# Five direct slots and a quarter-packed shared list in a sparse graph-network kernel

## The chip, the cores and the metric

The kernel runs on one core of one Trainium2 chip. The metric is device time in microseconds (us) from launch to end, the median of several runs. The engines are named as the profile names them: PE is TensorE (matrix multiply), PEld its weight loads, DVE VectorE, ACT ScalarE, POOL GpSimd, and SP the queue that issues most DMAs.

## The reference

There are 32 graphs of 512 nodes with 128 features. An adjacency entry is nonzero with chance 1/16, and always on the diagonal. Layer 0 is a normalized graph convolution with residual and layer norm. Layer 1 sums a message over every edge, and the message goes through a layer norm and an exact GELU of its own:

```python
m_j = jnp.einsum('bnd,do->bno', node_features, W1[:D])
m_i = jnp.einsum('bnd,do->bno', node_features, W1[D:])
pre = m_j[:, None, :, :] + m_i[:, :, None, :] + b1
msg = jax.nn.gelu(_layernorm(pre, g1, be1), approximate=False)
agg = jnp.einsum('bijo,bij->bio', msg, adjacency)
upd_in = jnp.concatenate([node_features, agg], axis=-1)
updated = _layernorm(upd_in @ W2 + b2, g2, be2)
```

The result is `_layernorm(x + updated)`. A term with a zero adjacency entry adds nothing, so the kernel computes messages of existing edges alone.

## The kernel before

One graph is one *block* of the program's main loop (not to be confused with a 128 x 128 tile of its adjacency matrix, of which a graph has 16, called *tiles* here). For a tile, each of the 128 rows on the partitions has about eight neighbours among 128 columns, four in each half of 64.

**Direct slots.** `lists` finds for each row and half the eight largest keys, with their indices. The first `SLOTS` = 4 of each half are *direct*: slot `t` of a half is one neighbour for every row. `gathered` brings the index rows into every partition by a broadcast DMA (`raw`), `gathers` turns them into a 0/1 matrix `s` on DVE, `turned` transposes that by DMA into `mt`. A *unit* `(t, q)` handles slot `t` of row chunk `q` against all four column chunks, both halves: 2 x 4 x 128 messages of 128 features.

**Shared places.** The neighbours beyond the direct ones (four kept per half, and up to eight more of the whole tile, found by `more`) are numbered through over the 128 rows of a tile. `counts` makes the running numbers, `spots` makes a 0/1 matrix `sj` that says which row owns which place, `sending` multiplies it with the tile's weights, indices and variances (`sent`), `picks` selects each place's entry and writes index rows to DRAM. A tile has `SHARED * P` = 256 places: two lots of 128. A shared unit handles two row chunks of one lot, 2 x 4 x 128 messages. If a tile had more entries than places, `flag` would be set and `dense_path` would redo the whole work.

**A unit's work.** `pairs` (PE) builds the pre-activation in PSUM (`u`, two buffers): gathers of the features in three bf16 parts (line 869 direct, 887 shared), the deviations times the bias (877, 890), and for shared units also the own rows through `sj` (884). For direct units `sums` (DVE, line 896) adds the own rows and moves the result to SBUF (`m`), which frees the PSUM buffer; for shared units ACT reads PSUM itself. `messages` (ACT, line 929) makes eight GELUs of 128 x 128, `weights` (POOL, lines 912 and 916) makes the weighted scatter matrix `sw`, and `aggregate` (PE, lines 943 and 953) adds the messages up in PSUM (`agg`).

**Order.** Nothing is scheduled by a tool: the order on each engine is the order in which the loop issues. It goes over units two by two. At an even unit `g` PE gets `pairs` of `g` and `g + 1`; at `g + 1` it gets `aggregate` of the two units before those. A block before has 20 units:

```python
order = [(t, q) for t in range(SLOTS - 1) for q in range(C)]
last, more_t = SLOTS - 1, (SLOTS, SLOTS + 1)
order += [(last, 0), (last, 1), (more_t[0], 0), (last, 2), (more_t[0], 1), (last, 3), (more_t[1], 0), (more_t[1], 1)]
```

All other work of a block (`layer0`, `parts`, `lists`, `factors`, `more`, `counts`, `spots`, `sending`, `picks`, `own_edges`, `finish`) is cut into steps by `yield`. `PLAN` gives each step's place by hand, counted in half units from the start of the block's first unit; negative places lie beside the units of the block before. `fetch` issues the DMAs: the index rows three units ahead of a slot's first unit, the compare and the deviation rows two ahead, the transpose one ahead. SP issues in order.

## Time and profile before

| | |
|---|---|
| median of 3 runs | 2945.51 us (2942.2 to 2951.59) |
| the profiled execution | 2950.83 us, span 2949.1 us |
| busy, share of the span | PE 94%, ACT 86%, DVE 83%, PEld 78%, POOL 72% |
| DMA, mean busy share of 16 engines | 42.3% on the main queue |
| mean granted TensorE clock | 0.987 |

The span is the time between the first and the last instruction. Busy shares are averages over the stages of a block; the profile repeats the same pattern for each of the 32 graphs. PE's matmuls overlap, so the time that one takes is best read from the start of a group to the start of the next in the timeline, and not from the mean duration of one.

### The profile page before, as it was taken

How to read it: one execution, taken by the hardware profiler on the slowest of the kernel's cores; microseconds unless marked ns; L12 is line 12 of the kernel's file. 1: busy time of each engine (PE TensorE's matmuls, PEld its weight loads, DVE VectorE, ACT ScalarE, POOL GpSimd, SP SyncE). 2: the span in 40 equal slices, each digit the busy share in tenths (PEclk: the TensorE clock that was granted, in tenths of full speed). 3: DMA queues.
4: the chain of work that ended last, by engine and by line, in shares of the span. 5: the costliest groups of instructions: out<-in, count | busy, mean ns of one | idle time of the engine just before them, and what ended most of it. 6: DMA issues, size and time to landing. Idle time of an engine off the chain costs nothing. (4 is left out here: it accounts for less than half of the span.)

```text
span 2949.1 us, 96041 instructions
## 1 busy us (share of the span) xinstructions
PE 2780.1 (94%) x35393; PEld 2314.2 (78%) x35393; DVE 2441.2 (83%) x9834; ACT 2540.1 (86%) x7841; POOL 2132.8 (72%) x2621
## 2 busy tenths in 40 slices
PE   4999999999999999999999999999999999999996
PEld 2788878788787788787888787788787888787885
DVE  5788988888988888988889888889888889888882
ACT  2888998888888888988888988888989888888885
POOL 3677877777877767776777777778777778776765
PEclk7999999999999999999999999999999999999998
DMA  1444444444443444434444434444434444434442
GB/s 43 91 93 105 103 101 79 99 91 107 106 97 75 93 99 102 109 82 89 100 102 102 101 79 99 93 108 103 101 79 99 89 109 106 100 79 96 91 97 48
DMA packets 593022, 276.09 MB, mean 94 GB/s; under 512 B 456112, under 2 KB 576048, under 8 KB 592544
## 3 DMA queue, kind: packets, MB, share of 16 engines
q1 hardware_dynamic: 592320, 269.41, 42.3%
q8 instruction: 281, 4.60, 0.6%
q14 instruction: 197, 1.61, 0.2%
q0 software_dynamic: 224, 0.46, 0.1%
HBM read 155.45 MB, written 13.63 MB: 57 GB/s over the span
## 5 line engine op out<-in xcount | busy, mean ns | idle before, releaser
L929 ACT ACTIVATE m<-m,r 128x128 f32<-128x128 f32 x4096 | 1267.4, 393 | 39.3 <-DVE m L896 39.3
L912 POOL TENSOR_TENSOR sw<-mt,a_t 128x512 f32<-128x512 bf16 x512 | 617.6, 1220 | 132.3 <-DMA mt<-s 74.1
L896 DVE TENSOR_TENSOR m<-u,ac 128x1024 f32<-128x1024 f32 x512 | 607.0, 1207 | 14.3 <-PE u L877 14.1
L943 PE MATMUL agg<-m,sw 128*64 128x128 f32 x8192 | 514.0, 277 | 5.6 <-ACT m L929 5.0
L943 PEld LDWEIGHTS agg<-m,sw 128*64 128x64 f32 x8192 | 442.7, 137 | 92.0 <-issue 45.5
L869 PEld LDWEIGHTS <-s 64*128 64x128 bf16 x12288 | 365.7, 95 | 138.3 <-issue 63.7
L869 PE MATMUL u<-c,s 64*128 64x128 bf16 x12288 | 434.0, 218 | 13.3 <-DVE s L832 12.7
L686 ACT COPY sent<-pl 128x328 f32<-128x328 f32 x512 | 221.4, 432 | 126.4 <-PE pl L690 66.9
L916 POOL TENSOR_TENSOR sw<-mt,sent 128x512 f32<-128x512 bf16 x256 | 291.3, 1161 | 9.0 <-PE agg L953 6.3
L690 PE MATMUL pl<-a_t,sj 128*128 128x164 f32 x2048 | 293.6, 304 | 0.0
L690 PEld LDWEIGHTS pl<-a_t,sj 128*128 128x128 f32 x2048 | 285.6, 190 | 8.5 <-DVE y L367 8.2
L929 ACT ACTIVATE m<-u,r_s 128x128 f32<-128x128 f32 x1024 | 279.0, 378 | 6.2 <-PE u L890 5.9
L884 PE MATMUL u<-ac,sj 128*128 128x128 f32 x2048 | 273.7, 277 | 0.0
L884 PEld LDWEIGHTS u<-ac,sj 128*128 128x128 f32 x2048 | 263.5, 191 | 12.0 <-DVE a_t L596 5.1
L953 PE MATMUL agg<-m,sw 128*128 128x128 f32 x2048 | 247.5, 277 | 0.0
L953 PEld LDWEIGHTS agg<-m,sw 128*128 128x128 f32 x2048 | 238.7, 192 | 9.2 <-POOL own_u L476 7.9
L887 PE MATMUL u<-c,s 128*128 128x128 bf16 x3072 | 213.3, 219 | 0.0
L523 DVE FIND_INDEX8 idx<-top,key 128x8 uint32<-128x64 f32 x1024 | 210.1, 218 | 0.0
L593 DVE MATCH_REPLACE8 key<-top,key 128x64 f32<-128x64 f32 x1024 | 205.0, 207 | 0.0
L741 POOL TENSOR_SCALAR ve_s<-picked 128x32 f32<-128x32 f32 x32 | 7.9, 248 | 262.0 <-DVE picked L727 262.0
L887 PEld LDWEIGHTS <-s 128*128 128x128 bf16 x3072 | 193.6, 98 | 3.0
L877 PE MATMUL u<-be_d,sd_rows 64*128 64x512 bf16 x1024 | 195.7, 378 | 0.0
(212 smaller groups left out, 5739.6 us busy)
## 6 DMA issues: line engine op xcount, KB each, us to landing
raw<-idx_d SPq DMA_DIRECT2D x256, 256.5 KB
raw<-idx_ds SPq DMA_DIRECT2D x64, 513.0 KB
a_nat<-in_adj_dram SPq DMA_DIRECT2D x32, 1024.0 KB
sd_rows<-sd_d SPq DMA_DIRECT2D x768, 12.0 KB
xs<-in_x_dram SPq DMA_DIRECT2D x32, 256.0 KB
out_dram<-o_sb SPq DMA_DIRECT2D x32, 256.0 KB
sd_d<-sd_p SPq DMA_DIRECT2D x256, 12.0 KB
mt<-s SPq DMA_TRANSPOSE x192
```

What stands on the lines that cost most here:

```text
L523: nc.vector.max_index(idx[:, to, h, :], top[:, to, h, :], half(to, h))
L686: nc.scalar.copy(sent[:, n - 1], pt[:, : SHARED * WIDE].rearrange("p (k w) -> p k w", w=WIDE))
L690: nc.tensor.matmul(pt[:, k * WIDE : (k + 1) * WIDE], sj[:, n, k * P : (k + 1) * P], at[:, n, :], start=True, stop=True,)
L869: nc.tensor.matmul(pu[:, h, c, :], s[halved(h), c, q * P : (q + 1) * P], c3[halved(h), k, c, :], start=(c == 0 and k == 0), stop=False,)
L884: nc.tensor.matmul(pu[:, h, c, :], place, st["ac"][:, q_h, 0, :], start=(c == 0), stop=False)
L887: nc.tensor.matmul(pu[:, h, c, :], s[:, c, q_h * P : (q_h + 1) * P], c3[:, k, c, :], start=False, stop=False)
L896: nc.vector.tensor_tensor(u.rearrange("p h c d -> p (h c) d"), pu.rearrange("p h c d -> p (h c) d"), bcast(state[b]["ac"][:, q, 0, :], 2 * C),
L912: nc.gpsimd.tensor_tensor(sw, mt[:, :, q, :], st["a_t"][:, q, :, :P], ALU.mult)
L916: nc.gpsimd.tensor_tensor(sw, mt[:, :, q_h, :], a, ALU.mult)
L929: nc.scalar.activation(m[:, h, c, :], u[:, h, c, :], AF.Gelu, scale=r[:, k : k + 1])
L943: nc.tensor.matmul(agg[halved(h), c, :], sw[0][:, c, halved(h)], m[:, h, c, :], start=(begin and c == 0), stop=(end and c == C - 1),)
L953: nc.tensor.matmul(agg[:, c, :], sw[h][:, c, :], m[:, h, c, :], start=False, stop=(end and h == 1 and c == C - 1),)
```

## The change

`SLOTS` becomes 5, so a block has 20 direct units. Three entries per half are kept beyond them; their groups stay four wide, the fourth place filled with a value that counts as empty. A tile has `PLACES` = 160 shared places: one full lot of 128 (slot `full`, two units as before) and 32 more (slot `rest`). The 32 places of four tiles lie side by side in the 128 columns of PE's array and become one column chunk; the four chunks make two units with two chunks each, a quarter of a unit's messages. A block has 24 units, and `PLAN` is rewritten for 48 half units.

```diff
-SLOTS = 4
+SLOTS = 5
 KEPT = LIST - SLOTS
-MORE = 2 * KEPT + LIST
-PARTS = MORE // KEPT
-SHARED = 2
+GROUP = 4
+MORE = 2 * GROUP + LIST
+PARTS = MORE // GROUP
+REST = 32
+PLACES = 128 + REST
...
-    "counts": [-3, -3, -2, -2, -2],
-    "own_edges": [7, 18, 22, 30],
-    "spots": [-2, -1, 0, 2, 3, 4, 6, 7, 7, 7],
-    "sending": [8, 9, 9, 9, 9, 9, 9, 9, 9, 9, 9, 9, 9, 9, 9, 9, 9],
-    "picks": [10, 12, 12, 14, 15, 18, 20, 20, 20, 20, 22, 23],
+    "counts": [-5, -1, -1, -1, 2],
+    "own_edges": [6, 10, 17, 32],
+    "spots": [-1, 0, 1, 2, 7, 8, 11, 13, 13, 17],
+    "sending": [20, 25, 25, 25, 25, 25, 25, 25, 25, 25, 25],
+    "picks": [28, 28, 28, 28, 29, 29, 30, 31, 31, 31, 32, 33],
...
+        for k in range(2):
+            pads = at[:, :, P + k * MORE : P + k * MORE + 2 * GROUP].rearrange("p n (h t) -> p n h t", h=2)
+            nc.gpsimd.memset(pads[:, :, :, KEPT:], NEG)
...
-        sj = big.tile([P, C * C, SHARED * P], F32, tag="sj", name=f"sj_{b}")
+        sj = big.tile([P, C * C, PLACES], F32, tag="sj", name=f"sj_{b}")
...
-        for n in range(C * C + 1):
+        for n in range(n_cols // 2 + 1):
             if n:
-                nc.scalar.copy(sent[:, n - 1], pt[:, : SHARED * WIDE].rearrange("p (k w) -> p k w", w=WIDE))
-            if n < C * C:
+                nc.scalar.copy(sent[:, 2 * n - 2 : 2 * n], pt[:, : 2 * WIDE].rearrange("p (k w) -> p k w", w=WIDE))
+            if n < n_cols // 2:
                 pt = bank(f"pl_{b}_{n}")
-                for k in range(SHARED):
...
+                for k in range(2):
+                    col = 2 * n + k
+                    here = slice(k * WIDE, (k + 1) * WIDE)
+                    if col < C * C:
+                        nc.tensor.matmul(pt[:, here], sj[:, col, :P], at[:, col, :], start=True, stop=True)
+                        continue
+                    for q in range(C):
+                        block = q * C + col - C * C
+                        nc.tensor.matmul(
+                            pt[q * REST : (q + 1) * REST, here], sj[:, block, P:], at[:, block, :],
+                            start=True, stop=True, tile_position=(0, q * REST),
+                        )
...
-    last, more_t = SLOTS - 1, (SLOTS, SLOTS + 1)
-    order += [(last, 0), (last, 1), (more_t[0], 0), (last, 2), (more_t[0], 1), (last, 3), (more_t[1], 0), (more_t[1], 1)]
+    last, full, rest = SLOTS - 1, SLOTS, SLOTS + 1
+    order += [(last, 0), (last, 1), (last, 2), (full, 0), (last, 3), (full, 1), (rest, 0), (rest, 1)]
...
+        if t == rest:
+            for c, col in enumerate((2 * q, 2 * q + 1)):
+                for q_h in range(C):
+                    nc.tensor.matmul(
+                        pu[q_h * REST : (q_h + 1) * REST, 0, c, :], st["sj"][:, q_h * C + col, P:],
+                        st["ac"][:, q_h, 0, :], start=(c == 0), stop=False,
+                        tile_position=(0, q_h * REST),
+                    )
+            for c, col in enumerate((2 * q, 2 * q + 1)):
+                for k in range(3):
+                    nc.tensor.matmul(pu[:, 0, c, :], s[:, col, :P], c3[:, k, col, :], start=False, stop=False)
+            nc.tensor.matmul(pu[:, 0, :2], dev[:, 0, :], be_s[:, 2 * q : 2 * q + 2], start=False, stop=True)
+            return pu
...
+            elif t == rest:
+                cols = mt.rearrange("p c q i -> p (c q) i")[:, 2 * q : 2 * q + 2, :]
+                nc.gpsimd.tensor_tensor(
+                    sw[:, :2], cols, st["sent"][:, C * C + 2 * q : C * C + 2 * q + 2, :P], ALU.mult
+                )
...
+        elif t == rest:
+            for c, col in enumerate((2 * q, 2 * q + 1)):
+                nc.tensor.matmul(
+                    agg[:, col, :], sw[0][:, c, :], m[:, 0, c, :], start=False, stop=(end and c == 1)
+                )
```

In `picks` the 32 columns of entries become 20 (16 tiles and four packed chunks). The other lines of `PLAN` are rewritten too: `layer0` begins at -53 instead of -43 and `more` ends at -6 instead of -5.

More of the change, by code (lines that the diff above doesn't have):

```diff
@@ L32 @@
 PLAN = {
-    "layer0": [-43, -41, -39, -39, -38, -37, -36, -34, -34, -33, -32, -31, -30, -30, -29, -28, -27, -27, -27, -27, -26, -24, -20, -18, -16, -3],
-    "lists": [-26, -26, -25, -24, -23, -20, -19, -19, -18, -18, -14, -13, -13, -13, -12, -12, -12, -11, -11, -10, -10],
-    "parts": [-20, -14, -12, -11, -6, -5, -4, -4, -4],
-    "factors": [-12, -11, -10, -8, -7, -7, -7, -6, -5],
-    "more": [-26, -25, -12, -10, -10, -10, -8, -7, -6, -6, -6, -5, -5, -5, -5, -5, -5, -5],
-    "counts": [-3, -3, -2, -2, -2],
-    "own_edges": [7, 18, 22, 30],
-    "spots": [-2, -1, 0, 2, 3, 4, 6, 7, 7, 7],
-    "sending": [8, 9, 9, 9, 9, 9, 9, 9, 9, 9, 9, 9, 9, 9, 9, 9, 9],
-    "picks": [10, 12, 12, 14, 15, 18, 20, 20, 20, 20, 22, 23],
-    "finish": [43, 44, 45, 50, 53, 55, 55, 60, 62, 69, 70, 79, 80],
+    "layer0": [-53, -51, -49, -49, -49, -47, -46, -45, -44, -43, -42, -42, -39, -39, -38, -37, -36, -36, -35, -35, -34, -27, -25, -24, -22, -5],
+    "lists": [-32, -32, -32, -23, -23, -20, -20, -18, -18, -18, -18, -18, -18, -18, -18, -16, -16, -13, -11, -9, -7],
+    "parts": [-10, -9, -8, -6, -4, -4, -4, -3, -2],
+    "factors": [-16, -15, -14, -14, -14, -13, -13, -12, -8],
+    "more": [-25, -25, -22, -14, -13, -13, -13, -11, -11, -11, -11, -10, -10, -7, -7, -7, -7, -6],
+    "counts": [-5, -1, -1, -1, 2],
[3 more added lines that the diff above has]
+    "picks": [28, 28, 28, 28, 29, 29, 30, 31, 31, 31, 32, 33],
+    "finish": [50, 53, 53, 55, 59, 60, 62, 64, 64, 67, 68, 72, 77],
 }
@@ L117, in sparse_path @@
     nc.gpsimd.iota(place_p, pattern=[[0, 1]], base=1, channel_multiplier=1, allow_small_or_imprecise_dtypes=True)
-    n_places = SHARED * P + 2
+    n_places = PLACES + 2
+    n_cols = C * C + C
     place_w = node.tile([P, 3, n_places // 3], F32, tag="t1", name="place_w")
@@ L139, in sparse_path @@
     nc.vector.tensor_add(step_down, step_down, ident_h)
-    place_k = const.tile([P, SHARED], F32, name="place_k")
-    nc.gpsimd.iota(
-        place_k, pattern=[[P, SHARED]], base=1, channel_multiplier=1, allow_small_or_imprecise_dtypes=True
-    )
-    own = slice(0, C * C, C + 1)
-    nth = const.tile([P, KEPT], F32, name="nth")
-    nc.gpsimd.iota(
-        nth, pattern=[[1, KEPT]], base=0, channel_multiplier=0, allow_small_or_imprecise_dtypes=True
+    place_r = const.tile([P, 1], F32, name="place_r")
+    nc.vector.tensor_copy(place_r, place_p)
+    above = const.tile([P, 1], F32, name="above")
+    for k in range(1, P // REST):
+        nc.vector.tensor_scalar(above, place_p, float(k * REST), None, ALU.is_gt)
+        nc.vector.tensor_scalar(above, above, -float(REST), None, ALU.mult)
+        nc.vector.tensor_add(place_r, place_r, above)
+    nc.vector.tensor_scalar(place_r, place_r, float(P), None, ALU.add)
+    own = slice(0, C * C, C + 1)
+    nth = const.tile([P, GROUP], F32, name="nth")
+    nc.gpsimd.iota(
+        nth, pattern=[[1, GROUP]], base=0, channel_multiplier=0, allow_small_or_imprecise_dtypes=True
     )
@@ L609, in counts @@
             nc.scalar.activation(
-                node_i[:, :, h * KEPT : (h + 1) * KEPT], idx[:, :, h, SLOTS:], AF.Copy, bias=float(h * HALF)
+                node_i[:, :, h * GROUP : h * GROUP + KEPT], idx[:, :, h, SLOTS:], AF.Copy, bias=float(h * HALF)
             )
-        nc.scalar.copy(node_i[:, :, 2 * KEPT :], st["idx_m"])
+        nc.scalar.copy(node_i[:, :, 2 * GROUP :], st["idx_m"])
+        for k in range(2):
+            pads = at[:, :, P + k * MORE : P + k * MORE + 2 * GROUP].rearrange("p n (h t) -> p n h t", h=2)
+            nc.gpsimd.memset(pads[:, :, :, KEPT:], NEG)
         nc.gpsimd.tensor_copy(
-            var[:, :, : 2 * KEPT].rearrange("p n (h t) -> p n h t", h=2), top[:, :, :, SLOTS:]
+            var[:, :, : 2 * GROUP].rearrange("p n (h t) -> p n h t", h=2)[:, :, :, :KEPT], top[:, :, :, SLOTS:]
         )
@@ L620, in counts @@
         nc.vector.tensor_reduce(
-            of_part, over.rearrange("p n (g t) -> p n g t", t=KEPT), AX.X, ALU.add
+            of_part, over.rearrange("p n (g t) -> p n g t", t=GROUP), AX.X, ALU.add
         )
@@ L669, in spots @@
                 nc.vector.tensor_copy(
-                    sj[:, 2 * k - 4 : 2 * k - 2, :], pt.pop(k - 2).rearrange("p (n e) -> p n e", n=2)
+                    sj[:, 2 * k - 4 : 2 * k - 2, :],
+                    pt.pop(k - 2)[:, : 2 * PLACES].rearrange("p (n e) -> p n e", n=2),
                 )
@@ L673, in spots @@
                 pt[k - 1] = bank(f"pj_{b}_{k}")
-                nc.tensor.matmul(pt[k - 1], step_down, up_to.pop(k - 1)[:, :, : SHARED * P], start=True, stop=True)
+                nc.tensor.matmul(
+                    pt[k - 1][:, : 2 * PLACES], step_down, up_to.pop(k - 1)[:, :, :PLACES], start=True, stop=True
+                )
             yield
@@ L681, in sending @@
         at = st["a_t"].rearrange("p q c w -> p (q c) w")
-        sent = big.tile([P, C * C, SHARED, WIDE], F32, tag="sent", name=f"sent_{b}")
+        sent = big.tile([P, n_cols, WIDE], F32, tag="sent", name=f"sent_{b}")
         st["sent"] = sent
-        for n in range(C * C + 1):
+        for n in range(n_cols // 2 + 1):
             if n:
-                nc.scalar.copy(sent[:, n - 1], pt[:, : SHARED * WIDE].rearrange("p (k w) -> p k w", w=WIDE))
-            if n < C * C:
+                nc.scalar.copy(sent[:, 2 * n - 2 : 2 * n], pt[:, : 2 * WIDE].rearrange("p (k w) -> p k w", w=WIDE))
+            if n < n_cols // 2:
                 pt = bank(f"pl_{b}_{n}")
-                for k in range(SHARED):
-                    nc.tensor.matmul(
-                        pt[:, k * WIDE : (k + 1) * WIDE],
-                        sj[:, n, k * P : (k + 1) * P],
-                        at[:, n, :],
-                        start=True,
-                        stop=True,
-                    )
+                for k in range(2):
[10 more added lines that the diff above has]
+                        )
             yield
@@ L702, in picks @@
         sent = st["sent"]
-        n_r = SHARED * C * C
-        rank = small.tile([P, SHARED, C * C, PARTS], F32, tag="rank", name=f"rank_{b}", bufs=1)
-        for k in range(SHARED):
+        n_r = n_cols
+        rank = small.tile([P, n_cols, PARTS], F32, tag="rank", name=f"rank_{b}", bufs=1)
+        for cols, place in ((slice(0, C * C), place_p), (slice(C * C, n_cols), place_r)):
             nc.vector.tensor_scalar(
-                rank[:, k], sent[:, :, k, P + 2 * MORE :], place_k[:, k : k + 1], -1.0, ALU.subtract, ALU.mult
+                rank[:, cols], sent[:, cols, P + 2 * MORE :], place, -1.0, ALU.subtract, ALU.mult
@@ L708, in picks @@
             )
-        chosen = node.tile([P, SHARED, C * C, MORE], BF16, tag="idx_r", name=f"chosen_{b}")
+        chosen = node.tile([P, n_cols, MORE], BF16, tag="idx_r", name=f"chosen_{b}")
         picked = small.tile([P, 2, n_r], F32, tag="picked", name=f"picked_{b}", bufs=1)
-        for k in range(SHARED):
-            nc.vector.tensor_tensor(
-                chosen[:, k].rearrange("p n (g t) -> p (n g) t", t=KEPT),
-                bcast(nth, C * C * PARTS),
-                rank[:, k].rearrange("p n g -> p (n g)").unsqueeze(2).to_broadcast([P, C * C * PARTS, KEPT]),
-                ALU.is_equal,
-            )
+        nc.vector.tensor_tensor(
+            chosen.rearrange("p n (g t) -> p (n g) t", t=GROUP),
+            bcast(nth, n_cols * PARTS),
+            rank.rearrange("p n g -> p (n g)").unsqueeze(2).to_broadcast([P, n_cols * PARTS, GROUP]),
+            ALU.is_equal,
+        )
@@ L718, in picks @@
         yield
         for h in range(2):
-            kept = node.tile([P, SHARED, C * C, MORE], F32, tag="xs", name=f"kept_{b}_{h}")
-            nc.vector.tensor_tensor(
-                kept,
-                chosen,
-                sent[:, :, :, P + h * MORE : P + (h + 1) * MORE].rearrange("p n k l -> p k n l"),
-                ALU.mult,
-            )
-            nc.vector.tensor_reduce(picked[:, h, :], kept.rearrange("p k n l -> p (k n) l"), AX.X, ALU.add)
+            kept = node.tile([P, n_cols, MORE], F32, tag="xs", name=f"kept_{b}_{h}")
@@ L728, in picks @@
+            nc.vector.tensor_tensor(kept, chosen, sent[:, :, P + h * MORE : P + (h + 1) * MORE], ALU.mult)
+            nc.vector.tensor_reduce(picked[:, h, :], kept, AX.X, ALU.add)
             yield
             if h == 0:
-                idx_h = small.tile([P, C, SHARED * C], BF16, tag="idx_s", name=f"idx_s_{b}", bufs=1)
-                for k in range(SHARED):
-                    nc.scalar.copy(
-                        idx_h[:, :, k * C : (k + 1) * C],
-                        picked[:, 0, k * C * C : (k + 1) * C * C].rearrange("p (q c) -> p q c", c=C),
-                    )
@@ L736, in picks @@
-        n_i = SHARED * C
+                idx_h = small.tile([P, C, C + 1], BF16, tag="idx_s", name=f"idx_s_{b}", bufs=1)
+                nc.scalar.copy(idx_h[:, :, :C], picked[:, 0, : C * C].rearrange("p (q c) -> p q c", c=C))
+                nc.scalar.copy(idx_h[:, :, C], picked[:, 0, C * C :])
+        n_i = C + 1
         pt = bank(f"pidx_s_{b}")
@@ L741, in picks @@
         nc.gpsimd.tensor_scalar(
-            ve.rearrange("p (k c q) -> p k q c", k=SHARED, c=C),
-            picked[:, 1, :].rearrange("p (k q c) -> p k q c", k=SHARED, c=C),
+            ve[:, : C * C].rearrange("p (c q) -> p q c", c=C),
+            picked[:, 1, : C * C].rearrange("p (q c) -> p q c", c=C),
             1.0 / D,
@@ L748, in picks @@
         )
+        nc.gpsimd.tensor_scalar(ve[:, C * C :], picked[:, 1, C * C :], 1.0 / D, EPS, ALU.mult, ALU.add)
         r = small.tile([P, n_r], F32, tag="r_s", name=f"r_s_{b}")
@@ L763, in picks @@
         n = C * C
-        sd_d = dram.tile([SHARED, 3, n, P], BF16, tag="sd_ds", name=f"sd_ds_{b}")
+        sd_d = dram.tile([3, n, P], BF16, tag="sd_ds", name=f"sd_ds_{b}")
+        sd_e = dram.tile([3, C, P], BF16, tag="sd_dr", name=f"sd_dr_{b}")
         yield
-        for k in range(SHARED):
-            nc.sync.dma_start(sd_d[k].rearrange("k n j -> n k j"), sd_p[k * n : (k + 1) * n])
+        nc.sync.dma_start(sd_d.rearrange("k n j -> n k j"), sd_p[:n])
+        nc.sync.dma_start(sd_e.rearrange("k n j -> n k j"), sd_p[n:])
+        st["sd_dr"] = sd_e
         st["sd_ds"] = sd_d
@@ L816, in gathered @@
             src, n0 = state[b]["idx_ds"], (t - SLOTS) * C
-        n = C * N + PAD
-        raw = onehot.tile([P, 3, n // 3 + 2], BF16, tag="raw", name=f"raw_{b}_{t}", bufs=1)
+        raw = onehot.tile([P, 3, (C * N + PAD) // 3 + 2], BF16, tag="raw", name=f"raw_{b}_{t}", bufs=1)
+        n = (N if t == rest else C * N) + PAD
         s = raw[:, :, : n // 3]
@@ L831, in gathers @@
         s = onehot.tile([P, C * N + PAD], BF16, tag="s", name=f"s_{b}_{t}", bufs=3)
+        n = N if t == rest else C * N
         nc.vector.tensor_scalar(
-            s.rearrange("p (k e) -> p k e", k=3), raw, node_h if t < SLOTS else node_p, None, ALU.is_equal
+            s[:, : n + PAD].rearrange("p (k e) -> p k e", k=3), raw, node_h if t < SLOTS else node_p, None, ALU.is_equal
         )
-        return s[:, : C * N]
+        return s[:, :n]
     def turned(b, t, s):
         mt = onehot.tile([P, C, C, P], BF16, tag="mt", name=f"mt_{b}_{t}", bufs=4)
-        nc.sync.dma_start_transpose(out=mt.rearrange("p c q i -> p (c q) i"), in_=s)
+        nc.sync.dma_start_transpose(out=mt.rearrange("p c q i -> p (c q) i")[:, : s.shape[-1] // P], in_=s)
         return mt
@@ L846, in deviations @@
         st = state[b]
-        srcs = [st["sd_d"][2 * t + h] for h in BOTH] if t < SLOTS else [st["sd_ds"][t - SLOTS]]
+        if t == rest:
+            for k in range(3):
+                nc.sync.dma_start(
+                    rows_t[k * DEV : (k + 1) * DEV, 0, :], st["sd_dr"].rearrange("k c j -> (k c) j")
+                )
+            return rows_t
+        srcs = [st["sd_d"][2 * t + h] for h in BOTH] if t < SLOTS else [st["sd_ds"]]
         for h, src in enumerate(srcs):
@@ L878, in pairs @@
             return pu
+        if t == rest:
+            for c, col in enumerate((2 * q, 2 * q + 1)):
[4 more added lines that the diff above has]
+                        tile_position=(0, q_h * REST),
+                    )
+            for c, col in enumerate((2 * q, 2 * q + 1)):
+                for k in range(3):
+                    nc.tensor.matmul(pu[:, 0, c, :], s[:, col, :P], c3[:, k, col, :], start=False, stop=False)
+            nc.tensor.matmul(pu[:, 0, :2], dev[:, 0, :], be_s[:, 2 * q : 2 * q + 2], start=False, stop=True)
+            return pu
         for h in BOTH:
             q_h = 2 * q + h
-            k = t - SLOTS
             for c in range(C):
-                place = st["sj"][:, q_h * C + c, k * P : (k + 1) * P]
+                place = st["sj"][:, q_h * C + c, :P]
                 nc.tensor.matmul(pu[:, h, c, :], place, st["ac"][:, q_h, 0, :], start=(c == 0), stop=False)
@@ L908, in weights @@
         out_w = []
-        for h in BOTH if t >= SLOTS else BOTH[:1]:
+        for h in BOTH if t == full else BOTH[:1]:
             sw = pair.tile([P, C, P], F32, tag="sw", name=f"sw_{b}_{t}_{q}_{h}", bufs=6)
@@ L912, in weights @@
                 nc.gpsimd.tensor_tensor(sw, mt[:, :, q, :], st["a_t"][:, q, :, :P], ALU.mult)
+            elif t == rest:
+                cols = mt.rearrange("p c q i -> p (c q) i")[:, 2 * q : 2 * q + 2, :]
+                nc.gpsimd.tensor_tensor(
+                    sw[:, :2], cols, st["sent"][:, C * C + 2 * q : C * C + 2 * q + 2, :P], ALU.mult
+                )
             else:
                 q_h = 2 * q + h
-                a = st["sent"][:, q_h * C : (q_h + 1) * C, t - SLOTS, :P]
+                a = st["sent"][:, q_h * C : (q_h + 1) * C, :P]
                 nc.gpsimd.tensor_tensor(sw, mt[:, :, q_h, :], a, ALU.mult)
@@ L923, in messages @@
         n = C * C
-        for c in range(C):
+        for c in range(2 if t == rest else C):
             if t < SLOTS:
                 r, k = st["r"], (t * 2 + h) * n + c * C + q
+            elif t == rest:
+                r, k = st["r_s"], n + 2 * q + c
             else:
-                r, k = st["r_s"], (t - SLOTS) * n + c * C + 2 * q + h
+                r, k = st["r_s"], c * C + 2 * q + h
             nc.scalar.activation(m[:, h, c, :], u[:, h, c, :], AF.Gelu, scale=r[:, k : k + 1])
@@ L949, in aggregate @@
                     )
+        elif t == rest:
+            for c, col in enumerate((2 * q, 2 * q + 1)):
+                nc.tensor.matmul(
+                    agg[:, col, :], sw[0][:, c, :], m[:, 0, c, :], start=False, stop=(end and c == 1)
+                )
         else:
@@ L970, in crowded @@
         nc.vector.tensor_reduce(peak, pt[:1, :P], AX.X, ALU.max)
-        nc.vector.tensor_scalar(flag, peak, SHARED * P + 0.5, None, ALU.is_gt)
+        nc.vector.tensor_scalar(flag, peak, PLACES + 0.5, None, ALU.is_gt)
     made_r, made_s, made_m, made_d = {}, {}, {}, {}
@@ L1020, in gather_two @@
             b, t, q = unit(k)
-            held[k] = pairs(b, t, q, made_s[b, t].rearrange("p (c j) -> p c j", j=N), made_d[b, t])
+            held[k] = pairs(b, t, q, made_s[b, t].rearrange("p (c j) -> p c j", c=C), made_d[b, t])
     def sum_one(k):
@@ L1062, in sparse_path @@
                 ready[k] = (u, m, sw)
-                work += [(key, u, m, h) for h in BOTH]
+                work += [(key, u, m, h) for h in (BOTH[:1] if key[1] == rest else BOTH)]
             if odd:
```

## The prediction

> **What bounds the kernel now.** First the page: who is busy, and whether anything but the steady repetition of blocks matters.

> ```profile
> span 2949.1 us, 96041 instructions
> PE 2780.1 (94%) x35393; PEld 2314.2 (78%) x35393; DVE 2441.2 (83%) x9834; ACT 2540.1 (86%) x7841; POOL 2132.8 (72%) x2621
> PE   4999999999999999999999999999999999999996
> ```

> PE is busy from end to end, at nearly full granted clock. The next view lists the instructions that write `agg_sb`, one for each block, and so gives the period: (2924.8 - 173.3) / 31 = 88.8 us.

> ```profile
> L775 DVE TENSOR_TENSOR agg_sb<-agg,own_u x32: 690/691/693, 173.3 to 2924.8; 128x512 f32<-128x512 f32 x32
> ```

> The windows view of one period shows each engine's load in it.

> ```profile
> 1000.00:1089.20 89.20, 85.55 (x1101) 71.04 (x1100) 76.44 (x306) 78.54 (x244) 65.54 (x81) 1.00 0.47 96
> ```

> The columns after the length are PE, PEld, DVE, ACT, POOL, clock, DMA share, GB/s. PE idles 3.65 us a block, ACT 10.7, DVE 12.8. PE sets the period. "Busy" alone could hide a stalled PE, so I read the starts in PE's timeline (start, duration, instructions):

> ```profile
> 1018.43 1.97 PE L943 MATMUL agg<-m,sw 128*64 128x128 f32 x32
> 1020.33 0.28 PE L760 MATMUL psd_s<-ident,sd_s 128*32 128x128 f32 x1
> ...
> 1050.79 1.05 PE L884 MATMUL u<-ac,sj 128*128 128x128 f32 x8
> ...
> 1052.56 1.05 PE L884 MATMUL u<-ac,sj 128*128 128x128 f32 x8
> ...
> 1054.34 1.95 PE L953 MATMUL agg<-m,sw 128*128 128x128 f32 x16
> 1056.22 1.09 PE L943 MATMUL agg<-m,sw 128*64 128x128 f32 x16
> ...
> 1079.34 0.84 PE L869 MATMUL u<-c,s 64*128 64x128 bf16 x24
> 1080.02 0.38 PE L877 MATMUL u<-be_d,sd_rows 64*128 64x512 bf16 x2
> 1080.23 0.83 PE L869 MATMUL u<-c,s 64*128 64x128 bf16 x24
> 1080.90 0.38 PE L877 MATMUL u<-be_d,sd_rows 64*128 64x512 bf16 x2
> 1081.21 9.18 PE L690 MATMUL pl<-a_t,sj 128*128 128x164 f32 x64
> 1090.32 1.86 PE L943 MATMUL agg<-m,sw 128*64 128x128 f32 x30
> ```

> The groups follow each other without a gap: PE really issues at its rate. From start to start, a direct unit costs 0.89 + 1.90/2 = 1.84, with its share of shape changes 1.9 us; a shared unit 2 x 1.77 (from L884 to the next half's L884) + 1.88 = 5.42 us; `sending` 9.11 us for 32 matmuls (0.285 each; the trace counts an f32 matmul as two).

> **The change, part by part, per block.**

> *PE.* Four more direct units: +7.6. Two shared units fewer: -10.84. The two quarter units: each has eight f32 matmuls of 32 columns, which the trace doesn't show. The nearest row is L943: 32 of 64 columns take the time of 16 full ones (1.90 against 1.88), so two half-wide ones run side by side. Bounds: four side by side, 2 x 0.22 = 0.45 us a unit, or one after the other, 8 x 0.22 = 1.78. I take the first, because of L943. With six bf16 (0.33), the deviation (0.2), two `aggregate` matmuls (0.47) and two shape changes (0.2) a unit costs 1.65, the two +3.3. `sending`: 16 full (4.56) and 16 quarter ones, 1.14 side by side or 4.56 in a row; with shape changes 5.9 instead of 9.11, -3.2. `spots` has 320 instead of 512 columns: eight at 0.31 shrink in proportion at most, -0.8. Sum **-3.9** us (+2.2 with every quarter matmul alone).

> A shape change is seen above: L869 follows L877 in 0.21 us, but L690, with other tiles of the array, follows in 0.31, so a change costs 0.1. [...]

> *ACT.* The rows (ACT's timeline gives 20 direct GELUs in 5.86 us from start to start, 0.293 each, and 16 shared ones in 4.02, 0.251 each):

> ```profile
> L929 ACT ACTIVATE m<-m,r 128x128 f32<-128x128 f32 x4096 | 1267.4, 393 | 39.3 <-DVE m L896 39.3
> L686 ACT COPY sent<-pl 128x328 f32<-128x328 f32 x512 | 221.4, 432 | 126.4 <-PE pl L690 66.9
> ```

> 32 more direct GELUs +9.4; 32 shared ones become 16 + 4, -3.0; 16 `sent` copies become ten, -2.6. **+3.8**.

> *DVE.* Four more L896 (607.0 us in 512) +4.7; one more compare (a quarter of one slot) +0.4; `spots` and `picks` shrink by 3/8 in width: between nothing and -5.0 (L661, L669, L712, L721 and L727, together 13.5 a block); fixed parts remain, so -3.7. **+1.4**.

> *POOL.* Four more L912 at 617.6 / 512 = 1.21, +4.8; eight L916 at 291.3 / 256 = 1.14 become four, -4.6; two of half width between 0.6 and 1.1 each, +1.2; the power on 32 columns (5.4 us; 1.05 on 4) becomes 20 columns, -1.9; two memsets and one extra op +0.6. **+0.1**.

> *DMA and SP.* One more transpose of a quarter, index rows 3.1 to 3.2 MB, 36 instead of 30 deviation issues. At a share of 0.47 this is no bound by itself, but see the rivals.

> Window sums after: PE 81.6, ACT 82.3, DVE 77.8, POOL 65.6. The bound falls from 85.55 to 82.3, 3.2 us. But before, one engine led; afterwards PE and ACT are level, and the engine that is longer changes along the block. So I added the rows pair of units by pair of units, in the order of issue (PE, ACT, DVE, POOL, in us; DVE's last pairs are one entry, halved here; small waits are in PE's rows):

> ```
> before  0  8.5 10.6  7.6  6.4    after  0  4.9 10.0  7.2  9.7
>         1 10.3  7.7  9.2 10.1           1 10.3  5.2  6.1  6.8
>         2 15.5 13.8  7.2  4.1           2  6.8  6.8  6.0  4.6
>         3 10.7  9.8  8.5 10.0           3  8.8  9.1  5.8  4.1
>         4  5.3  4.7  5.5  4.6           4  3.9  5.2  5.0  6.1
>         5  6.1  6.3  6.8  7.2           5  6.9  4.7  5.2  4.1
>         6  4.8  5.2  8.5  3.9           6  9.0 10.6  9.5  3.9
>         7  7.4  8.8  7.4  9.4           7  4.4  6.3  8.6  7.6
>         8  7.4  6.0  7.7  5.6           8  4.1  9.3  7.7  5.2
>         9 11.0  6.0  7.7  4.8           9  9.1  5.0  6.6  2.4
>                                        10  7.4  5.7  4.9  3.4
>                                        11  7.4  4.8  4.9  8.1
> ```

> PSUM's two `u` buffers and five `m` buffers let engines drift apart by a pair or two, so waits even out over some stretch. Taking the largest engine sum in each stretch, averaged over where the cuts fall: with half blocks 88.5 before and 86.7 after; with thirds 90.6 and 88.1. Their mean, 89.55 before, is 0.75 above the measured 88.8; after it is 87.4, or 86.65 with 0.75 taken off. With fifths the sums are 91.4 and 92.4, which speaks against a gain, so I choose a value between, a period of 87.1, **1.7 us less**.

> Start and end (72.8 us until the first unit, the last block's finish) hold the same chains. 32 x 1.7 = 54: the span goes from 2949.1 to 2895. The profiled execution (2950.83) lies 5.3 above the median, so the median goes to 2945.5 - 54 = **2891**.

> **The rivals.** *POOL and the transpose at the seam of two blocks: slower.* There DMA is full (share 1.07 from 1057 to 1069 us: adjacency load, index rows, transpose), and `mt` comes late, in POOL's timeline

> ```profile
> 1066.04 2.30 POOL L912 TENSOR_TENSOR sw<-mt,a_t 128x512 f32<-128x512 bf16 x2 [5.27 <-DMA mt<-s]
> ```

> and in the list of waits, with total, times and longest:

> ```profile
> POOL sw L912 <- DMA mt<-s: 74.1, 18, 6.2
> ```

> Before, pairs 9, 0, 1 give PE 29.8 against POOL's 21.3: the wait, 4.1 on the mean, is covered. After, pairs 11, 0, 1 give PE 22.6, ACT 20.0, and POOL 24.6: no cover. If 4.1 come on every block the period is 91.2, the time 3022; half of it, 2957. It decides from 1.7 us a block. For it: the last pair before the seam is now the two quarter units. Against it: SP may issue earlier than the loop's place, and POOL has slack in pairs 9 and 10.

> *The quarter matmuls don't run side by side: slower.* +6.1 on PE, 87.7 in the window, with the 3.65 idle of before 91.35 against 89.2: 2945.5 + 32 x 2.15 = 3014. L943 speaks against it.

> *The engines even out fully: faster.* 82.3 and no more idle time than the 3.65 of before, 85.95 against 89.2: 2945.5 - 32 x 3.25 = 2841.

> *The alternation eats all: no change.* The fifths say this: 2945.

> That a tile overflows its places, and `dense_path` runs, I exclude: counted from the inputs, the fullest tile needs 142 of 160 places (253 of 256 before).

> **Chances.** Forecast 0.46, evening out 0.12, no change 0.10, seam 0.24, no packing 0.08. Run-to-run spread is 0.3%, about 9 us, which separates faster and slower from no change. The no-change case falls 0.02 to each side, so faster 0.60, same 0.06, slower 0.34. The range reaches from 2830, under the evening-out case, to 3000, into the seam case; the forecast's own range is 2855 to 2930.

> **What would show it.** Right: a period near 87, ACT and PE both near 82 busy, `sending` near 5.9 us from start to start, four quarter matmuls starting within some 0.11 us. Wrong: POOL's wait for `mt` above 1.7 us a block with PE waiting for `sw` (seam); quarter matmuls 0.1 us apart (no packing); PE and ACT waiting in turn for L896 and each other, period near 89 (alternation).

## The result, and the profile after

The changed kernel takes 3042.27 us (median of 4 runs, 3038.05 to 3051.49) against 2946.56 us before on the same chip: 1.0328 times the time, 95% interval 1.0312 to 1.0344. The prediction said 2891, faster; the time lies above its range. The profiled execution took 3041.32 us.

The page's engine line and the instructions that write `agg_sb` (first and last start give the period):

```profile
span 3039.5 us, 104394 instructions
...
PE 2740.4 (90%) x38785; PEld 2194.3 (72%) x38785; DVE 2506.4 (82%) x9973; ACT 2652.4 (87%) x8289; POOL 2128.5 (70%) x2780
```
```profile
L786 DVE TENSOR_TENSOR agg_sb<-agg,own_u x32: 672/678/693, 173.6 to 3015.2; 128x512 f32<-128x512 f32 x32
```

(3015.2 - 173.6) / 31 = 91.7 us a block, 2.9 more than before. The windows view, summed over 24 stretches of one steady block each, first before (89.12 us), then after (92.26 us; the last block is shorter, so the mean of all is 91.7):

```profile
sum 2138.88, PE 2069.09 PEld 1726.73 DVE 1823.55 ACT 1902.12 POOL 1592.22; mean PE 86.21 PEld 71.95 DVE 75.98 ACT 79.25 POOL 66.34
```
```profile
sum 2214.24, PE 2039.77 PEld 1635.04 DVE 1870.52 ACT 1983.67 POOL 1588.58; mean PE 84.99 PEld 68.13 DVE 77.94 ACT 82.65 POOL 66.19
```

ACT, DVE and POOL have the loads that were forecast (82.3, 77.8, 65.6), yet no engine is busy for more than 85 of 92.3 us. Before, PE was at work for all but 2.9 of 89.1. PE's timeline shows what is new (start, duration, instructions, idle time before and what ended it):

```profile
1049.69 3.05 PE L706 MATMUL pl<-a_t,sj 128*128 128x164 f32 x20 [0.26 <-ACT sent L699]
1052.67 1.32 PE L710 MATMUL pl<-a_t,sj 128*32 128x164 f32 x32
1053.92 1.97 PE L980 MATMUL agg<-m,sw 128*64 128x128 f32 x32
...
1061.83 0.28 PE L769 MATMUL psd_s<-ident,sd_s 128*20 128x128 f32 x1 [3.20 <-POOL sd_s L762]
1062.04 3.58 PE L980 MATMUL agg<-m,sw 128*64 128x128 f32 x32
```

The quarter matmuls (L710) run side by side as forecast (sixteen in 1.25 us from start to start). But PE stands for 3.2 us until POOL has made `sd_s`, and the next L980 takes 3.58 instead of 1.97 us. The windows view of four stretches of 3.41 us around it gives the reason (the columns are as in the prediction; the last three are the granted clock, the DMA share, GB/s):

```profile
1055.18:1058.59 3.41, 2.93 (x70) 2.16 (x66) 3.27 (x7) 3.41 (x14) 1.04 (x3) 1.00 0.01 2
1058.59:1062.00 3.41, 0.21 (x2) 0.09 (x1) 3.41 (x25) 2.42 (x8) 3.33 (x3) 1.00 0.10 21
1062.00:1065.41 3.41, 3.41 (x33) 3.28 (x32) 3.41 (x35) 3.23 (x13) 2.50 (x4) 0.50 1.02 216
1065.41:1068.82 3.41, 3.41 (x82) 2.88 (x80) 2.54 (x6) 3.36 (x8) 3.21 (x5) 1.00 0.27 88
```

After a window with PE almost idle (0.21 of 3.41 us busy) the granted clock is 0.50 for one window. PE's waits, first before and then after (total, times, longest):

```profile
PE po L634 <- DVE count_h L626: 31.6, 32, 1.0
PE pidx L534 <- ACT idx_h L528: 24.3, 30, 8.4
```
```profile
PE psd_s L769 <- POOL sd_s L762: 102.6, 32, 3.6
PE pconv L367 <- POOL a_t L330: 30.4, 30, 1.6
PE u L914 <- ACT m L966: 29.6, 31, 1.0
PE pt_x L269 <- ACT x L257: 27.9, 32, 4.9
```

All of PE's waits that come at least ten times add up to 97.5 us before and 234.9 after: 3.05 and 7.34 us a block. Time at half clock is 81 us before, nearly all at the two ends, and 205 after: (205 - 81) / 32 = 3.9 us a block at half rate, 1.9 lost if PE is busy in it, as in the third window above. So, by difference, 88.8 was 85.7 of work and 3.05 of waits; 91.7 is 82.4 of work, 7.34 of waits, 1.9 of clock. The work fell by 3.3, and 6.2 came back as waits and clock.

### The profile page after: what moved, and what is told of

It is laid out like the page before. It is cut to its first block, busy times and chain, and to the rows that moved or that the text cites. A ratio compares the mean times of both kernels' runs of the same rounds, so it can differ in the third digit from the quotient of the medians.

```text
span 3039.5 us, 104394 instructions
## 1 busy us (share of the span) xinstructions
PE 2740.4 (90%) x38785; PEld 2194.3 (72%) x38785; DVE 2506.4 (82%) x9973; ACT 2652.4 (87%) x8289; POOL 2128.5 (70%) x2780
## 3 DMA queue, kind: packets, MB, share of 16 engines
q1 hardware_dynamic: 630080, 279.98, 42.7%
## 5 line engine op out<-in xcount | busy, mean ns | idle before, releaser
L966 ACT ACTIVATE m<-m,r 128x128 f32<-128x128 f32 x5120 | 1571.2, 392 | 48.5 <-DVE m L926 46.6
L926 DVE TENSOR_TENSOR m<-u,ac 128x1024 f32<-128x1024 f32 x640 | 769.2, 1214 | 116.3 <-PE u L895 114.9
L942 POOL TENSOR_TENSOR sw<-mt,a_t 128x512 f32<-128x512 bf16 x640 | 739.1, 1166 | 170.3 <-DMA mt<-s 131.9
L980 PE MATMUL agg<-m,sw 128*64 128x128 f32 x10240 | 695.7, 289 | 1.6 <-POOL sw L942 1.0
L980 PEld LDWEIGHTS agg<-m,sw 128*64 128x64 f32 x10240 | 597.3, 144 | 91.7 <-issue 41.9
L844 DVE TENSOR_SCALAR s<-raw,node_h 128x2052 bf16<-128x2052 bf16 x160 | 202.8, 1268 | 96.2 <-DMA raw<-idx_d 80.7
L526 DVE MAX8 top<-key 128x8 f32<-128x64 f32 x1024 | 170.0, 210 | 1.1
L706 PEld LDWEIGHTS pl<-a_t,sj 128*128 128x128 f32 x1024 | 144.3, 190 | 35.7 <-ACT sent L699 18.8
L914 PE MATMUL u<-ac,sj 128*128 128x128 f32 x1024 | 141.6, 281 | 29.7 <-ACT m L966 29.6
L914 PEld LDWEIGHTS u<-ac,sj 128*128 128x128 f32 x1024 | 129.2, 191 | 50.5 <-ACT m L966 40.4
L367 PE MATMUL pconv<-s,a_t 128*128 128x128 f32 x1024 | 129.4, 281 | 32.6 <-POOL a_t L330 30.4
```

The source lines that it names most:

```text
L526: nc.vector.max(top[:, seq[n], h, :], half(seq[n], h))
L706: nc.tensor.matmul(pt[:, here], sj[:, col, :P], at[:, col, :], start=True, stop=True)
L844: nc.vector.tensor_scalar(s[:, : n + PAD].rearrange("p (k e) -> p k e", k=3), raw, node_h if t < SLOTS else node_p, None, ALU.is_equal)
L914: nc.tensor.matmul(pu[:, h, c, :], place, st["ac"][:, q_h, 0, :], start=(c == 0), stop=False)
L926: nc.vector.tensor_tensor(u.rearrange("p h c d -> p (h c) d"), pu.rearrange("p h c d -> p (h c) d"), bcast(state[b]["ac"][:, q, 0, :], 2 * C),
L942: nc.gpsimd.tensor_tensor(sw, mt[:, :, q, :], st["a_t"][:, q, :, :P], ALU.mult)
```

## The experiments

I followed the changed kernel's twelve blocks from the 14th to the 25th back from wait to wait, with the rule of the profile's chain of waits. Us of one block on the chain:

```
          PE    ACT   POOL   DVE   DMA   of
before   39.2   11.5   4.3   26.9   3.2   88.8
after    18.8   30.0  18.8   12.7   8.5   92.3
```

The rest, some 3.6 us, is SP's issuing and time in which the engine waited for nothing that the profile shows. The shares move by a microsecond or so with the way in which a wait is cut. The same hand-overs come in twelve blocks of twelve: `sent` (ACT), rank, chosen, kept, picked (DVE), the power for `r_s` (POOL, 3.56 us); from there the chain goes to `psd_s` (PE) in ten and on to ACT in eight. At the seam they are POOL's chain to `xb`, DVE's layer norm, POOL's power, ACT's `x`, PE's `pt_x`, again in all twelve. The theories tested: **D**, such serial chains, with queues in order on every engine, set the period; **P** and **A1**, PE or ACT alone does; **the seam**, as in the prediction's first rival; **the clock**.

All runs are given as ratio to the kernel before on the same chip; a difference of 0.01 is 0.92 us a block. Intervals are about 0.002 wide on each side. The changed kernel stands at 1.0328.

**PE's wait and the wait for `mt`.** In three runs the wait for `psd_s` was moved or filled, in a fourth POOL's step behind the wait for `mt` was moved (in e1 the steps of `picks` behind `psd_s` move by up to one half unit too):

```
 e1   yield  before the transpose psd_s, "picks": [28, 28, 28, 28, 29, 29, 31, 31, 32, 32, 32, 33, 33]
 e2   the same yield,                    "picks": [28, 28, 28, 28, 29, 29, 30, 30, 31, 31, 31, 32, 33]
 e3   + for _ in range(12): nc.tensor.matmul(pt, ident_h, be_d..., start=True, stop=True)   # ahead of psd_s
 e4   layer0's step that holds deg ... xb: place -46 -> -47
```

> The changed kernel with one step cut in two: the transpose of the shared deviations (psd_s) stands two half units later (place 31 instead of 29), behind the rows of indices, which stay. Theory A (a new wait: PE stands 3.2 us a block at that transpose, until POOL has made the power of 20 columns, and the clock is halved for a window behind it, which stretches the next aggregate from 1.97 to 3.58 us): both go, 32 x 4.8 = 155 us less, about 2890 us, granted clock back from 0.967 to about 0.985. Theory B (POOL and the late transposed matrices at the seam of two blocks, 131.9 us of waits): no change of more than 10 us, 3042. Theory C (PE and ACT take turns and no place helps): the wait comes back elsewhere, above 3000.

> The same, with the transpose only one half unit later (place 30). Theory A: half a unit is about 1.9 us, so some 1.3 us of the wait are left, too short to halve the clock for long: 32 x 3.5 = 112 us less, about 2930 us. If the clock's part did not belong to the wait, it would be 32 x 1.9 = 61 us less, 2980. Theory B: 3042. Theory C: above 3000.

> The changed kernel with twelve more matmuls of 128 x 512 (bf16, overwritten by the transpose, results unused) in the place where PE waits. They add 2.6 us of work inside a wait of 3.2 us. Theory A in two parts: if idling is what halves the clock, the wait stays and the clock does not fall: 32 x 1.6 = 51 us less, about 2990 us, and the aggregate behind it takes 1.97 us again. If the slow aggregate has another cause, no change, 3042. Theory B: no change. If PE had no time to spare there, 32 x 2.6 = 83 us more.

> The changed kernel with one step of layer0 one half unit earlier (the degree chain on POOL, place -47 instead of -46), so that it stands ahead of the block's first scatter matrix in POOL's order and no longer waits with it for the late transpose. Theory B: what the late transpose costs goes, up to 4.1 us a block, 131 us less, 2911. Theory A: at most the 1.0 us a block that PE waits at the convolution for POOL, 3010 to 3042.

Measured: e1 1.0481, e2 1.0305, e3 1.0349, e4 1.0304. In e2 and e3 the clock is back (110 and 74 us at half rate in all), PE's page time is down to 2720 us in e2, and nothing is gained. In e2 the wait has moved on:

```profile
PE psd L573 <- ACT sd L565: 53.4, 32, 12.8
PE psd_s L770 <- POOL sd_s L762: 41.8, 32, 1.7
PE agg L981 <- POOL sw L943: 36.0, 51, 0.9
```

So in the changed kernel this wait of PE is a symptom; what holds POOL and ACT up stays. e1 lost 1.4 us a block. In its trace SP's issue of the shared deviations waits for ACT for 185.9 us in all instead of 71.0, and PE waits for ACT ahead of `aggregate` for 50.4 us; that these are the cause isn't shown. e4's 0.2 us a block lies within the two intervals: holding `deg` up is at most a small part of what POOL's wait for `mt` costs.

**The loads.** GELUs and matmuls left out:

```
 f1   GELU of half 1, column 3 left out in slots 1 and 2 (8 a block)     h1   in slots 0 to 4 (20)
 f2   for k in range(3) -> range(2) at L887 in slots 1 and 2 (64)        h2   in slots 0 to 4 (160)
 h3   h1 and h2 together
```

> Leaves out 8 of the 160 direct GELUs of a block (half 1, column 3 of slots 1 and 2), 2.34 us of ACT by its row of 0.293 us each; nothing else changes. Theory D (a chain through several engines): followed back from wait to wait over twelve blocks of the changed kernel, the chain lies on ACT for 30.0 us of 92.3, on PE for 18.8, on POOL for 18.8, on DVE for 12.7, in DMA for 8.5; GELUs hold 19.4 us of it, of some 52 us of GELUs in a block, so 37% of what is left out comes back, 0.9 us a block, 28 us, near 3014. Theory P (PE still sets the period, through its own waits): nothing comes back, 3042. Theory A1 (ACT alone is the bound): all comes back, 75 us, near 2967.

> Leaves out the third of the three bf16 matmul terms of the same two slots (64 matmuls a block), 8 units of 0.28 us, 2.24 us of PE; ACT, DVE, POOL and DMA do the same as before. Theory D: these matmuls hold 2.05 us of the chain of 17.8 us in a block, 12%, so 0.3 us a block comes back, 8 us, near 3034. Theory P: all 2.24 us, 72 us, near 2970. Theory A1: nothing.

> As the run with 8 GELUs left out, now in all five direct slots: 20 GELUs a block, 5.9 us of ACT. Theory A1 (ACT is the bound): 5.9 us a block, 188 us, near 2854. Theory P (PE is the bound): nothing, 3042. Theory D (the chain goes back and forth between engines that are all busy for 78 to 85 us of 92, and shortening one leaves a parallel chain through the others): a part, 0 to 1.8 us a block, 2984 to 3042.

> Leaves out the third bf16 term in all five direct slots: 160 matmuls, 5.6 us of PE a block. Theory P: 179 us less, near 2863. Theory A1: nothing. Theory D: close to nothing, 0 to 1 us a block, 3010 to 3042.

> Both omissions at once, 5.9 us of ACT and 5.6 us of PE a block. Theory P: the 5.6 us of PE, no more than with PE's omission alone; theory A1: the 5.9 us of ACT, no more than with ACT's alone. Theory D: clearly more than the two single effects added, since the two parallel chains get shorter together: 3 to 5 us a block, 2880 to 2945.

Measured: f1 1.0322, f2 1.0324, h1 1.0284, h2 1.0317, h3 1.0204. So 5.9 us less on ACT give 0.4 us a block, 5.6 less on PE give 0.1, both 1.1. P and A1 are refuted; D is right in kind (more together than one by one), but not in size: f1 gave 0.06 us a block where 0.9 was expected, and h3 gave less than 3 to 5. In f1 the chain followed back lies on PE for about 30 us and on ACT for under 14 at an unchanged 92.2: several chains are nearly as long as the longest.

**The chains.** The transfer at the seam, and POOL's power:

```
 f3   a_nat kept from the first block; later blocks load [:, 0:1] of it (256 of 1024 KB)
 i1   - rsqrt(r, ve)
      + nc.gpsimd.tensor_copy(r[:, : C * C], ve[:, : C * C])
      + rsqrt(r[:, C * C :], ve[:, C * C :])
 i2   f3 and i1 together
```

> Loads only a quarter of the adjacency (256 of 1024 KB) in every block but the first, so that the transfer that stands ahead of the seam's transpose in the queue takes some 0.9 instead of 3.4 us; the rest keeps the first block's values, and no engine's work changes. Theory D: the load's landing holds 3.2 us of the chain and the transpose behind it 2.3; up to 2.5 us a block comes back, 0.9 if the next chain is that close, so 28 to 80 us, 2962 to 3014. Theories P and A1: nothing, since neither PE nor ACT has less to do.

> Leaves out the power for 16 of the 20 columns of r_s (a copy stands there), so that the step of 3.56 us on POOL, which lies on the chain in twelve blocks of twelve, takes about 1.4 us; ACT, PE, DVE and DMA have the same work, and POOL, busy 66 us of 92, is not short of time. Theory D (serial chains that pass through several engines set the period): a part of the 2.2 us comes back, 0.5 to 2 us a block, 2980 to 3026. Theory L (loads set it: whatever is left is one engine's busy time): nothing, 3042.

> The omission in r_s and the quarter of the adjacency together. The adjacency alone gave 1.35 us a block back (3042 to 3000). Theory D: both chains follow each other in a block, so the effects add or nearly: 2 to 3.3 us a block, 2936 to 2980. Theory L: as the adjacency alone, 3000.

Measured: f3 1.0175, i1 1.0263, i2 1.0120: 1.4, 0.6 and 1.9 us a block. Both chains count, the effects add (2.0 by sum), and no engine but POOL has less to do; i1's whole cut of POOL's step is 2.3 us (3.55 to 0.19 + 1.03) of an engine that idles for 26. SP's waits (after, then f3) and POOL's show one way in which the transfer costs:

```profile
SPq L852 <- DMA a_nat<-in_adj_dram: 84.6, 30, 4.4
...
POOL sw L942 <- DMA mt<-s: 131.9, 51, 9.4
```
```profile
SPq L853 <- DMA a_nat<-in_adj_dram: 13.9, 30, 1.6
...
POOL sw L943 <- DMA mt<-s: 83.5, 51, 9.9
```

The transpose of the new block's first slot is held on SP until the adjacency has landed, in 30 blocks of 32, 2.8 us each. A second way is ACT's own wait for the adjacency (`mask`), 26.6 us after and 10.6 in f3; f3 doesn't part the two.

The hold itself is not new. SP's timeline at the seam, before and then after:

```profile
1055.72 0.51 SPq L273 DMA_DIRECT2D a_nat<-in_adj_dram  x1
...
1056.87 5.13 SPq L840 DMA_TRANSPOSE mt<-s  x1
```
```profile
1085.55 0.40 SPq L280 DMA_DIRECT2D a_nat<-in_adj_dram  x1
...
1093.05 2.04 SPq L852 DMA_TRANSPOSE mt<-s  x1
```

Before, the transpose is issued 1.1 us behind the load and stands on SP itself for 5.1 us where most others take 1.8 to 2.0; in 30 of 31 blocks it ends within 0.1 us of the load's landing. After, it is the eighth DMA issued behind the load in 30 blocks, and SP waits ahead of it for the semaphore that the load counts up. What the hold cost the kernel before, no run shows.

**The clock.** h3 has the clock down for 341 us. With e3's twelve matmuls in it:

> The run with 20 GELUs and 160 matmuls left out a block (3010), with twelve matmuls of no use added where PE waits for psd_s, as in the earlier run with them, so that the clock stays up. That run had 59 windows at half clock, 341 us in all; the kernel before has 81 us of them at its two ends, so (341 - 81) / 32 = 8.1 us a block at half rate, 4.1 us of PE time. If the clock's windows ate what the lighter engines freed: up to 3 us a block, 2915 to 2980. If they lie off the chain: 3010.

Measured: 1.0090 against h3's 1.0204, 1.05 us a block, with 122 us at half clock. The mean clock and span of h3, then of this run:

```profile
core 0: 3014.8 us, clock 0.944
```
```profile
core 0: 2966.2 us, clock 0.980
```

So the halved clock took away part of what the lighter engines had freed. In e3, with the changed kernel's full work on ACT, the same fillers gave nothing.

**One place in the kernel before.** Only the step with the index rows' way to DRAM and `psd_s` moves, three half units earlier:

```
 e5   (kernel before)  picks: [10, 12, 12, 14, 15, 18, 20, ...] -> [10, 12, 12, 14, 15, 15, 20, ...]
```

> The kernel before, with nothing changed but the place of the transpose psd_s, which stands right behind POOL's power as in the changed kernel instead of one step of the plan later. Theory D with the clock gate: PE comes to wait there some 3 us in each block, the window behind is granted half the clock (38 such windows in the changed kernel, 7 in the kernel before), and 2 to 4 us a block are lost, 3010 to 3075, near what the whole change lost. Rival: the wait is filled up elsewhere in the block, 2947.

Measured: 1.0242, 2.2 us a block, though no work changed. The size is as expected, the way is not: PE hardly waits for `psd_s` (7.8 us in all), and the clock stays up (83 us at half rate in all). SP's timeline, before and then with the move, shows another queue:

```profile
1003.08 1.77 SPq L840 DMA_TRANSPOSE mt<-s  x1
1004.90 1.82 SPq L823 DMA_DIRECT2D raw<-idx_d  x2
1016.08 0.28 SPq L497 DMA_DIRECT2D idx_ds<-idx_rs  x1
...
1020.93 2.97 SPq L840 DMA_TRANSPOSE mt<-s  x1
```
```profile
1023.01 1.72 SPq L840 DMA_TRANSPOSE mt<-s  x1
1036.01 0.27 SPq L497 DMA_DIRECT2D idx_ds<-idx_rs  x1
...
1036.62 1.24 SPq L823 DMA_DIRECT2D raw<-idx_d  x2
...
1043.06 1.90 SPq L840 DMA_TRANSPOSE mt<-s  x1
```

The index rows' DMA waits for ACT (SP's L497 behind `m`: 338.4 us in all, 301.5 before) and stands ahead of `raw` now; the next `raw` goes out 13.6 instead of 1.8 us after the transpose, and from transpose to transpose it is 20.05 instead of 17.85 us: the 2.2 us. In the blocks from the 6th to the 28th this stretch is 20.17 instead of 17.84 us on the mean, and no other stretch between two transposes of a block changes by more than 0.4. PE has the same work and the largest load as ever, and one place is enough to let a chain through SP set the period.

**Other places.** Three sets of places for the changed kernel, with the same instructions (nearly every row of `PLAN` changed by a few half units; the third set's `picks` as an example):

```
 k1   "picks": [28, 28, 28, 28, 29, 29, 30, 31, 31, 31, 32, 33] -> [28, 28, 28, 29, 29, 30, 31, 31, 32, 33, 33, 33], ...
```

> The changed kernel with other places in the plan and nothing else: the same instructions, moved by one to eight half units, found by replaying each engine's queue in order with the durations of the two traces and keeping moves that shorten the period. Theory D: the loss sits in the waits between in-order queues, so other places bring it back; the replay, which gives 90.2 us a block for the changed kernel and 87.8 for the kernel before, gives 85.7 here, so 2830 to 2920. Theories P and A1: as much work on PE and on ACT as before, 3042 or close to it.

> The changed kernel with a second set of places, from the replay with its durations corrected by the runs so far (it now gives 92.2 us a block for the changed kernel, 87.8 for the kernel before, which measured 88.8, and 90.9 for the first set of places, which measured 92.2). For this set it gives 88.3. Theory D: 1.5 to 3.9 us a block less than the changed kernel, 2915 to 2995, the upper part the likelier since the replay was too low by 1.3 for the first set. Theories P and A1: 3042.

> The changed kernel with a third set of places, found with the clock's windows in the replay (a window of 3.41 us in which PE is busy for less than half is followed by one at half clock). The replay gives 87.1 us a block, 1.1 less than for the second set, which measured 90.8. Theory D: 1 to 3 us a block less than the changed kernel, 2945 to 3010. If no set of places helps further: near 3018, the second set's time. Should it come out under 2945, it beats the kernel before.

Measured: g1 1.0299, g2 1.0223, k1 1.0244. The best set brings 1.0 us a block back; all three stay behind what I expected of them, and none beats the kernel before. The replay (each engine's queue run through in order, with durations from the traces) had said 85.7, 88.3 and 87.1 us a block before they ran; 92.2, 91.5 and 91.5 were measured in the steady part. So it did not see a large part of what holds these orders up, and which part stays open. In g2 POOL's wait for `mt` is nearly gone:

```profile
POOL sw L951 <- DMA mt<-s: 5.9, 3, 5.0
```

That is 5.9 us in all, against 131.9 on `sw` L942 alone, and still only 1.0 us a block came back.

**All omissions.**

```
 l1   i2, h3 and the twelve matmuls of no use together
```

> All the omissions at once: 20 GELUs and 160 matmuls a block, the power for 16 columns, three quarters of the adjacency, and the twelve matmuls of no use. Theory D with its parts following each other in the block: the 2973 of the run with GELUs, matmuls and fillers less the 59 that power and adjacency gave (3042 to 2983), near 2915. If a load that none of them touches (DVE, 78 us of busy time a block) sets a floor: no lower than 2950.

Measured: 2914.38 us, 0.9894 (0.9872 to 0.9916), 4.0 us a block under the changed kernel. j3 and i2 by themselves gave 2.2 and 1.9. So chains, loads and clock add up in the changed kernel, and DVE at 77.84 us of busy time a block of 88.08 isn't the floor yet.

## Why the prediction was wrong

*PE's work.* Right within some 0.6 us. Predicted -3.9 a block, about -3.3 by the difference above. From the starts: a quarter unit 1.12 us plus its share of `aggregate`, 1.6 (predicted 1.65); `sending` 6.3 (5.9); a pair of direct units as before. Sixteen quarter matmuls take 1.25 us where 1.14 was predicted side by side and 4.56 in a row; in groups of four they start 7 ns apart, so the trace is near full packing.

*ACT, DVE, POOL.* Right: 82.65, 77.94 and 66.19 where 82.3, 77.8 and 65.6 stood.

*The step that failed* is the one from loads to period: "PSUM's two `u` buffers and five `m` buffers let engines drift apart by a pair or two, so waits even out over some stretch". Sums over half and third blocks gave 86.65, and with an eye on the fifths I chose 87.1; 91.7 was measured. The sums hold only how long each engine is busy in a stretch. They have no term for a chain that passes from engine to engine inside it, with each engine's queue standing behind the instruction that waits. The runs show such chains at work: 0.6 us a block come back from a step of POOL, which idles for 26 us (i1), 1.4 from a transfer (f3), and 0.4 and 0.1 from 5.9 us of ACT and 5.6 of PE (h1, h2). Before, PE waited for 3.05 us a block. That a full queue of PE covered the chains there, and that the level loads took this cover away, is argued from the waits; it is not shown, since none of the omissions was made in the kernel before. Nor do the runs part level loads from badly chosen places: three other sets brought at most 1.0 us back, and one place costs the kernel before 2.2.

The fifths, which I named and set aside, said 92.4, near the 91.7, but that is luck. The 92.4 comes of cutting twelve pairs into stretches of two and three; cut evenly, the printed rows give 91.3 after and 91.4 before, so the fifths said "no change". The halves and thirds after, averaged over all cuts as before was, are 86.3 and 87.7 instead of 86.7 and 88.1; this is small beside the miss.

*The clock* was left out of the sum. It is 1.9 us a block of PE's time by the trace. Keeping it up with matmuls of no use gave 1.05 us a block in the kernel with lighter ACT and PE (j3) and nothing in the changed kernel itself (e3).

*The seam rival* (0.24) had the right sign, and its time, 3022, was the nearest of all. Its wait has the priced 131.9 / 32 = 4.1 us a block by chance: it came 51 times with 2.6 us each, not once a block with 4.1. And its mechanism was at most a part. Not all of the wait is on the chain: the adjacency's landing is worth 1.4 us a block (f3), not the 4.1 that I reckoned; the wait hardly reaches PE as `sw` (1.0 us in all); and without it g2 is still slow. *Alternation* came near in kind, engines that wait in turn, but it named PE and ACT alone, and I let it stop at no change, with nothing in the profile that set that limit. *Evening out* is refuted by PE's 7.34 us of waits, *no packing* by L710.

In the changed kernel the adjacency's landing is worth 1.4 us a block, POOL's power 0.6, and other places 1.0. Whether these are parts of the 4.6 us between 87.1 and 91.7 isn't shown, since the kernel before has the same load and a longer power (5.4 us). How the 4.6 us divide among the nearly equal chains stays open.

## What to carry to other kernels

When a change makes several engines nearly equally busy, don't take busy sums for a forecast: follow the waits back through a steady block, and count each serial chain with what stands behind it in every queue it passes, SP's too. An engine that leads, as PE did before with 86.2 us busy a block against ACT's 79.3, may cover such chains (argued here, not shown), but one badly placed issue is enough to uncover one (e5, 2.2 us a block). Here 3.3 us of PE's work were saved, and 6.2 came back as waits and clock. Test an engine's lead by leaving a known amount of its work out, alone and together with a rival's.

## What the runs showed of the hardware

In both kernels the first transpose behind the adjacency load of 1 MB was held on SP, though DMA as a whole was busy for less than half of the time (42.3% on the main queue before, 42.7% after). In the kernel before, its issue itself took 5.1 us and in 30 of 31 blocks ended within 0.1 us of the load's landing; in the changed kernel SP waited 2.8 us a block ahead of it for the landing, 84.6 in all, and with a load of 256 KB 13.9 (f3).
